# Attention layer of a two-layer graph network: the normalised rows are summed by the attention weights first, W is applied to the sums, and s is formed from the rows and W's row sums on VectorE

## The chip, the cores and the metric

The kernel runs on one NeuronCore of a Trainium2 chip. The core has five engines, each with its own in-order queue of instructions: TensorE (PE in the profile; matmuls and transposes, with weight loads shown as PEld), VectorE (DVE), ScalarE (ACT), GpSimd (POOL) and SyncE (SP, which here only issues loads). Engines wait for one another on semaphores. The metric is the device time of the whole program in microseconds, the median of the runs.

## What is computed

The input x has 128 graphs of 128 nodes with 256 features, all in float32, and adj gives each graph's 128 x 128 adjacency as integers. Two layers follow each other, both with a normalisation ahead and a residual sum behind:

```
h = relu(layernorm(x));  x = x + GRU_layers(h, adj)      # layer 0
h = relu(layernorm(x));  x = x + attention(h, adj, W)    # layer 1
```

Layer 0 repeats a gated update three times: messages h @ weight[i] are summed over neighbours (A transposed), and a GRU cell combines the sums with h. Layer 1 is

```
Wh      = h @ W
s       = Wh.sum(axis=-1)
e       = leaky_relu(s[:, :, None] + s[:, None, :], 0.2);  e = -inf where adj == 0
alpha   = softmax(e, axis=-1)
h_prime = alpha @ Wh
```

The kernel uses that alpha @ Wh can have its division by the softmax's denominator at the end, together with the residual sum.

## The kernel before

Graphs are worked on in groups of G = 4, so there are 32 groups. A group's data is kept in two layouts: rows (nodes on the partitions) and T (features on the partitions, in KD = 2 halves of 128). `normed` (L137) normalises four 128 x 256 row blocks: statistics on VectorE, the reciprocal root on GpSimd (L145, L146), the scaling on VectorE (L149). `rows_to_T` (L153) and `T_to_rows` (L175) transpose on TensorE, eight transposes each. `aggregate` (L185) sums rows over neighbours and leaves the sum in T layout; VectorE evicts it. `gru_half` (L207) computes one half of the new state: four gate sums in PSUM, of twelve 512-wide matmuls, then sigmoid and tanh on ScalarE and five operations on VectorE, the last of which writes hT (L226). W of the three message layers is folded into the gate weights ahead of the loop.

`group` (L228) is a generator: it yields after each step of a group, and 16 steps make a group. Step 11 (L253 to L257) forms x1, the input of the attention layer, and normalises it; step 12 transposes it with the Relu in the eviction; step 13 multiplies by W, evicts the product `wh` with ScalarE and reduces it to s; step 14 (L266 to L283) builds the scores and the softmax; step 15 transposes the weights to eT; step 16 forms the output and stores it.

Two streams take the even and the odd groups. The first is started LAG = 7 steps early; then each is advanced by one step in turn (L309 to L316), so that the vector work of one stream's attention falls beside the gate matmuls of the other. From the code in that sequence the framework's scheduler makes the order of each engine's queue when the program is built: it moves instructions past each other where their data allow it. On the chip each queue then runs in that order. PSUM has five buffers for gates and three for everything else, `ps_misc` (L57); the tiles of the pool `work` have three buffers unless a number is given. Loads go through SyncE's queue two groups ahead, stores through GpSimd's.

## Time and profile before

| | |
|---|---|
| median of 3 runs | 2614.0 us (2613.59 to 2614.19) |
| profiled execution | 2614.36 us, of which 2612.6 us lie between the first and the last instruction (the span) |
| TensorE busy | 2547.0 us, 97% of the span |
| VectorE busy | 1282.0 us, 49% |
| ScalarE busy | 720.8 us, 28% |
| GpSimd busy | 104.1 us, 4% |
| mean granted TensorE clock | 0.994 of full |

In a row of the page or of the groups, the text ahead of the bar names the line, the engine, the operation, what it writes and reads (`out<-in`) with shapes, and how often it occurs; behind the bar stand the busy time in us and the mean duration of one in ns, and then the idle time of the engine just ahead of these instructions with what ended it. In a timeline a row gives the start and length in us, the engine, the line, the operation and how many were merged, and in brackets the idle time ahead of it and what ended that. In a table of stretches, each row gives a stretch, its length, the busy time and count of PE, PEld, DVE, ACT and POOL, the granted clock, the share of the DMA engines and GB/s. A float32 matmul leaves two records, a transpose one. The ends of matmuls are modelled, and neighbouring matmuls overlap in the records.

### The profile page before, as it was taken

Reading aid. Unit: us, or ns where it says so; the run is one execution under the profiler, and the core shown is the slowest. Engines: PE = TensorE matmul, PEld = TensorE weight load, DVE = VectorE, ACT = ScalarE, POOL = GpSimd, SP = SyncE. Lnnn points to the kernel's source line nnn. Section 1 sums busy time; section 2 is a strip of 40 time slices with the busy share of each in tenths; the row PEclk is TensorE's granted clock in tenths of the full one; section 3 lists DMA queues with packets and bytes.
Section 4 is the critical chain, followed back from the end, with each engine's and each line's share of the span. In section 5 each row is a group of like instructions: output and inputs, shape, how many; then the busy total and the mean of one; then the engine's idle time right before and its main releaser. Section 6 shows DMA issues by size and latency. Waiting matters only on the chain.

```text
span 2612.6 us, 22325 instructions
## 1 busy us (share of the span) xinstructions
PE 2547.0 (97%) x8532; PEld 1357.0 (52%) x8532; DVE 1282.0 (49%) x2487; ACT 720.8 (28%) x1063; POOL 104.1 (4%) x166
## 2 busy tenths in 40 slices
PE   6999999999999999999999999999999999999996
PEld 4455555555555555555555555555555555555553
DVE  3355454555545455454554545555454554545544
ACT  1223222332222322222232223322223222222322
POOL 0000000000000000000000000000000000000000
PEclk9999999999999999999999999999999999999998
DMA  3000000000000000000000000000000000000000
GB/s 101 1 21 21 9 21 20 15 18 12 17 21 21 13 21 13 16 21 13 20 21 9 21 21 15 19 13 17 21 21 12 21 9 16 17 9 8 9 1 17
DMA packets 42700, 46.01 MB, mean 18 GB/s; under 512 B 3168, under 2 KB 38496, under 8 KB 42592
## 3 DMA queue, kind: packets, MB, share of 16 engines
q1 hardware_dynamic: 33792, 25.17, 3.2%
q0 software_dynamic: 4608, 16.78, 1.8%
q10 hardware_dynamic: 4192, 2.63, 0.4%
q8 instruction: 67, 1.10, 0.2%
q14 instruction: 41, 0.34, 0.0%
HBM read 27.79 MB, written 16.78 MB: 17 GB/s over the span
## 4 chain that ended last, share of the span: by engine, by line
PE 87%; DVE 6%; issue 2%; ACT 2%; POOL 1%; DMA 1%; ACTq 0%; POOLq 0%; DVEq 0%
PE gate L203 69%; PE misc L191 7%; PE misc L170 4%; PE misc L181 3%; PE misc L294 2%; DVE h L149 1%; DVE bn_st L141 1%; POOL rstd L146 1%; PE misc L159 1%; ACT z L222 1%; DVE hT L226 1%; DVE d L225 1%; ACT L222 1%; PE misc L268 1%; PE misc L128 0%
## 5 line engine op out<-in xcount | busy, mean ns | idle before, releaser
L203 PE MATMUL gate<-hT,w_hhT 128*128 128x512 f32 x2304 | 1096.5, 593 | 0.0
L203 PE MATMUL gate<-aT,w_x 128*128 128x512 f32 x2304 | 1093.5, 596 | 0.0
L203 PEld LDWEIGHTS gate<-aT,w_x 128*128 128x128 f32 x2304 | 427.4, 190 | 553.7 <-issue 477.5
L203 PEld LDWEIGHTS gate<-hT,w_hhT 128*128 128x128 f32 x2304 | 419.2, 191 | 431.3 <-issue 407.2
L215 DVE SCALAR_TENSOR_TENSOR u<-gate,bias_h,r 128x512 f32<-128x512 f32 x192 | 144.0, 750 | 417.7 <-PE gate L203 417.7
L212 ACT ACTIVATE r<-gate,bias_s 128x512 f32<-128x512 f32 x192 | 132.1, 688 | 726.0 <-PE gate L203 726.0
L219 ACT ACTIVATE n<-u,bias_i 128x512 f32<-128x512 f32 x192 | 138.8, 723 | 610.8 <-DVE u L217 540.8
L225 DVE TENSOR_TENSOR d<-d,z 128x512 f32<-128x512 f32 x192 | 132.6, 691 | 238.1 <-ACT z L222 236.5
L222 ACT ACTIVATE z<-gate,bias_s 128x512 f32<-128x512 f32 x192 | 131.8, 687 | 272.4 <-PE gate L203 271.0
L191 PEld LDWEIGHTS misc<-a,rows 128*128 128x128 f32 x1536 | 185.4, 193 | 17.4 <-issue 11.6
L224 DVE TENSOR_TENSOR d<-hT,n 128x512 f32<-128x512 f32 x192 | 131.9, 687 | 124.0 <-ACT n L219 123.9
L191 PE MATMUL misc<-a,rows 128*128 128x128 f32 x1536 | 188.4, 276 | 0.0
L217 DVE TENSOR_TENSOR u<-u,gate 128x512 f32<-128x512 f32 x192 | 131.3, 684 | 116.2 <-PE gate L203 115.8
L193 DVE COPY aT<-misc 128x512 f32<-128x512 f32 x192 | 130.0, 684 | 40.0 <-PE misc L191 39.7
L181 PE MATMUL misc<-ident,hT 128*128 128x128 f32 x768 | 119.9, 278 | 22.1 <-DVE hT L226 16.9
L226 DVE TENSOR_TENSOR hT<-n,d 128x512 f32<-128x512 f32 x192 | 132.3, 689 | 4.4
L181 PEld LDWEIGHTS misc<-ident,hT 128*128 128x128 f32 x768 | 87.6, 141 | 75.4 <-DVE hT L226 48.3
L170 PE MATMUL misc<-w,h1T 128*128 128x256 f32 x512 | 121.6, 386 | 0.6 <-ACT h1T L160 0.5
L170 PEld LDWEIGHTS misc<-w,h1T 128*128 128x128 f32 x512 | 95.7, 192 | 24.8 <-issue 7.2
L250 ACT COPY rows<-misc 128x512 f32<-128x512 f32 x128 | 69.1, 591 | 100.7 <-PE misc L181 100.7
L262 DVE TENSOR_REDUCE s<-wh 128x4 f32<-128x1024 f32 x32 | 39.0, 1220 | 109.3 <-ACT wh L172 109.3
L300 POOL DMA_DIRECT2D out_dram<-o x32 | 25.6, 802 | 1296.7 <-DVE o L297 1259.5
(60 smaller groups left out, 1201.1 us busy)
## 6 DMA issues: line engine op xcount, KB each, us to landing
xt<-in_x_dram SPq DMA_DIRECT2D x32, 512.0 KB, 3.9
out_dram<-o POOLq DMA_DIRECT2D x32, 512.0 KB, 3.4
at<-in_adj_dram SPq DMA_DIRECT2D x32, 256.0 KB, 2.8
w_msg<-in_L_gnn_weight_dram ACTq DMA_DIRECT2D x1, 768.0 KB, 7.0
w_hh_nat<-in_L_gnn_w_hh_dram ACTq DMA_DIRECT2D x1, 768.0 KB, 10.6
w_ih_nat<-in_L_gnn_w_ih_dram ACTq DMA_DIRECT2D x1, 768.0 KB, 13.8
w<-in_L_gnn_W_dram ACTq DMA_DIRECT2D x1, 256.0 KB, 9.0
bias_i<-in_L_gnn_b_ih_dram ACTq DMA_DIRECT2D x1, 3.0 KB, 11.8
```

The lines of the kernel that those rows point to most:

```text
L170: nc.tensor.matmul(ps[:, b, :], srcT[:, k, (b0 + b) * N:(b0 + b + 1) * N], w[:, k, :], start=(k == 0), stop=(k == KD - 1))
L181: nc.tensor.transpose(ps[:, b, k * P:(k + 1) * P], srcT[:, k, (b0 + b) * N:(b0 + b + 1) * N], ident)
L191: nc.tensor.matmul(ps[:, b * N:(b + 1) * N], m[:, b, k * P:(k + 1) * P], a[:, b, :], start=True, stop=True)
L203: nc.tensor.matmul(ps, w[:, k, c * P:(c + 1) * P], t[:, k, :], start=(i == 0), stop=(i == n - 1))
L212: nc.scalar.activation(r, p_r, AF.Sigmoid, bias=bias_s[:, cr:cr + 1])
L215: nc.vector.scalar_tensor_tensor(u, p_hn, bias_h[:, cn:cn + 1], r, op0=OP.add, op1=OP.mult)
L217: nc.vector.tensor_tensor(u, u, p_in, OP.add)
L219: nc.scalar.activation(n, u, AF.Tanh, bias=bias_i[:, cn:cn + 1])
L222: nc.scalar.activation(z, p_z, AF.Sigmoid, bias=bias_s[:, cz:cz + 1])
L224: nc.vector.tensor_tensor(d, hT[:, j, :], n, OP.subtract)
L225: nc.vector.tensor_tensor(d, d, z, OP.mult)
L226: nc.vector.tensor_tensor(new[:, j, :], n, d, OP.add)
```

## The change

At the start the sums of W's rows over its outputs, `w1_out`, are reduced on VectorE, and transposed and copied into `w1_sum`, which holds them in a row on all partitions. In the attention layer h1 gets its Relu in place on ScalarE and is no longer transposed; s is formed on VectorE, graph by graph, as the sum over a row of h1 times `w1_sum`. After the softmax, `aggregate` sums the rows of h1 by eT and leaves the sums in T layout, and `rows_product` multiplies those by W straight into the PSUM tile that the output step reads. The step that transposed h1 and the step that formed `wh` are gone, the summing is a step of its own, and s joins the step of the normalisation: 15 steps make a group. The numbers of the lines behind the change move up by 7 or so.

```diff
+    w1_out = const.tile([P, KD], F32, name="w1_out")
+    nc.vector.tensor_reduce(w1_out, w1, AX.X, OP.add)
+    w1_sum = const.tile([P, D], F32, name="w1_sum")
+    ps = ps_misc.tile([P, 512], F32, name="misc")
+    for k in range(KD):
+        nc.tensor.transpose(ps[:, k * P:(k + 1) * P], w1_out[:, k:k + 1].to_broadcast([P, P]), ident)
+    nc.scalar.copy(w1_sum, ps[:, :D])
...
-    def rows_to_T(src, name, bufs, func=AF.Copy):
+    def rows_to_T(src, name, bufs):
...
-            nc.scalar.activation(dst[:, k, :], ps[:, :GN], func)
+            nc.scalar.copy(dst[:, k, :], ps[:, :GN])
...
-    def rows_product(srcT, w, name):
-
-        dst = work.tile([P, G, D], F32, name=name)
-        for b0 in range(0, G, 2):
-            ps = ps_misc.tile([P, 2, D], F32, name="misc")
-            for b in range(2):
-                for k in range(KD):
-                    nc.tensor.matmul(ps[:, b, :], srcT[:, k, (b0 + b) * N:(b0 + b + 1) * N],
-                                     w[:, k, :], start=(k == 0), stop=(k == KD - 1))
-            nc.scalar.copy(dst[:, b0:b0 + 2, :], ps)
-        return dst
+    def rows_product(srcT, w, b0):
+
+        ps = ps_misc.tile([P, 2, D], F32, name="misc")
+        for b in range(2):
+            for k in range(KD):
+                nc.tensor.matmul(ps[:, b, :], srcT[:, k, (b0 + b) * N:(b0 + b + 1) * N],
+                                 w[:, k, :], start=(k == 0), stop=(k == KD - 1))
+        return ps
...
-        h = normed(x1, "h")
-        yield
-        h1T = rows_to_T(h, "h1T", 2, AF.Relu)
-        yield
-        wh = rows_product(h1T, w1, "wh")
+        h1 = normed(x1, "h")
+        nc.scalar.activation(h1, h1, AF.Relu)
         s = small.tile([P, G], F32, name="s")
-        nc.vector.tensor_reduce(s, wh, AX.X, OP.add)
+        for b in range(G):
+            hw = work.tile([P, D], F32, name="hw")
+            nc.vector.scalar_tensor_tensor(hw, h1[:, b, :], 1.0, w1_sum, op0=OP.mult, op1=OP.mult,
+                                           accum_out=s[:, b:b + 1])
         yield
...
         nc.scalar.copy(eT, p_e)
         yield
+
+        hT = aggregate(h1, eT)
+        yield
         o = work.tile([P, G, D], F32, name="o")
         for b0 in range(0, G, 2):
-            ps = ps_misc.tile([P, 2, D], F32, name="misc")
-            for b in range(2):
-                nc.tensor.matmul(ps[:, b, :], eT[:, b0 + b, :], wh[:, b0 + b, :],
-                                 start=True, stop=True)
+            ps = rows_product(hT, w1, b0)
```

## The prediction

> **What bounds the kernel now.** I read the page's busy shares first, then its groups.

> ```profile
> PE 2547.0 (97%) x8532; PEld 1357.0 (52%) x8532; DVE 1282.0 (49%) x2487; ACT 720.8 (28%) x1063; POOL 104.1 (4%) x166
> ...
> L203 PE MATMUL gate<-hT,w_hhT 128*128 128x512 f32 x2304 | 1096.5, 593 | 0.0
> ...
> L262 DVE TENSOR_REDUCE s<-wh 128x4 f32<-128x1024 f32 x32 | 39.0, 1220 | 109.3 <-ACT wh L172 109.3
> ```

> TensorE (PE) is busy almost throughout, VectorE (DVE) half the time. So time is PE's work plus PE's stalls. The 593 ns overlap each other; the spacing comes from the timeline of PE:

> ```profile
> 1242.51 1.04 PE L181 MATMUL misc<-ident,hT 128*128 128x128 f32 x8
> 1243.39 1.88 PE L203 MATMUL gate<-hT,w_hhT 128*128 128x512 f32 x4
> 1245.11 1.88 PE L203 MATMUL gate<-aT,w_x 128*128 128x512 f32 x4
> ...
> 1257.33 0.87 PE L181 MATMUL misc<-ident,hT 128*128 128x128 f32 x6 [0.97 <-DVE hT L226]
> 1258.04 3.19 PE L170 MATMUL misc<-w,h1T 128*128 128x256 f32 x14
> 1261.07 1.95 PE L191 MATMUL misc<-a,rows 128*128 128x128 f32 x16
> ...
> 1362.84 1.89 PE L294 MATMUL misc<-wh,eT 128*128 128x256 f32 x8
> 1364.57 0.27 PE L181 MATMUL misc<-ident,hT 128*128 128x128 f32 x1
> ...
> 1415.95 0.87 PE L181 MATMUL misc<-ident,hT 128*128 128x128 f32 x6 [0.97 <-DVE hT L226]
> ```

> From start to start: eight transposes 0.87 us, four 512-wide records 1.72 (0.429 each; a matmul leaves two records), 16 records of L191 1.78, eight of L294 1.73, L170's 14 3.03 (0.216 each). The same stall stands at 1257.33 and 1415.95: two groups take 158.62 us, one 79.31.

> PE's work per group: gates 144 x 0.429 = 61.8; L191 3 x 1.78 = 5.3; L181 3 x 0.87 = 2.6; L159 2 x 0.87 = 1.7; L170 3.45; L294 1.73; L268 and L286 0.87. Sum 77.5, so stalls cost 1.8 per group.

> What decides the changed kernel is DVE at that stall, from its timeline:

> ```profile
> 1243.15 0.69 DVE L254 TENSOR_TENSOR x<-xt,misc 128x512 f32<-128x512 f32 x1 [1.64 <-PE misc L181]
> ...
> 1248.66 1.38 DVE L149 TENSOR_SCALAR h<-x,bn_mv,rstd 128x256 f32<-128x256 f32 x4 [1.12 <-POOL rstd L146]
> 1249.96 0.75 DVE L215 SCALAR_TENSOR_TENSOR u<-gate,bias_h,r 128x512 f32<-128x512 f32 x1
> ...
> 1253.97 0.41 DVE L149 TENSOR_SCALAR h<-xt,bn_mv,rstd 128x256 f32<-128x256 f32 x1 [1.40 <-POOL rstd L146]
> ...
> 1256.59 0.69 DVE L226 TENSOR_TENSOR hT<-n,d 128x512 f32<-128x512 f32 x1
> ```

> One stream's normalisation stands in DVE's queue ahead of the other stream's GRU update. That update's hT ends 14.77 us after the transposes of x1 began (1257.28 less 1242.51), though its gate sums were done at 11.2. Before, 3.8 us of attention work filled the time.

> [...] L273 reads one f32 tile twice and takes 683 ns, as a plain tensor_tensor (688)[...]. [...] after 3.36 idle us before 46.30 the clock column (after POOL's) fell.

> ```profile
> 46.00:48.00 2.00, 1.70 (x14) 1.71 (x15) 1.99 (x7) 1.25 (x3) 0.00 (x0) 0.89 0.03 8
> 48.00:50.00 2.00, 2.00 (x11) 2.00 (x11) 0.69 (x1) 1.36 (x2) 0.00 (x0) 0.50 0.59 163
> 50.00:52.00 2.00, 2.00 (x7) 1.10 (x7) 0.69 (x1) 0.00 (x0) 0.00 (x0) 0.76 0.77 230
> ```

> [...]

> **The change part by part.** *PE work.* Gone: eight transposes of h1 (0.87) and L294 (1.73). Added: a second aggregation of 16 records (1.78). The product with W (3.45) moves behind it. Net -0.82: 76.7 per group, -26 us in all.

> *ScalarE (ACT) work.* Four evictions of 0.59 go, one Relu of 1.07 comes; ACT is 28% busy, so only its place counts.

> *DVE work.* The reduction (1.22) goes; two evictions of 0.69 and four weighted row sums come. A row sum: 128x256 takes 0.41 alone (L149), each waits for the one before (dependent steps are 0.72 apart for 0.69 of work, so 0.03), and I add 0.08 for the accumulator read (the small aggregations follow each other at 0.07). 0.52 each, 2.08 together. Bounds: 1.6 (overlapped, 0.33 + 0.07)[...].

> *Order.* A group now has 15 steps in place of 16, with the lag at 7, so the streams pair anew. In the built order (what each engine's queue of the changed kernel holds) every group has the same stretch on PE: eight transposes of x1; a gate half of the other stream (10.30); four transposes of s; two transposes and four gate records that need only the first half of the other stream's hT; six transposes that need its second half; four gate records; four transposes of e; the aggregation. The product that used to stand there is gone. DVE's order there: x1, statistics, h, u of L215, row sums, L217, rest of the next group's statistics, its h, e plus the row of s, d times z, e plus the column, hT, then the rest of the softmax. The queues of SyncE and GpSimd keep their order, with the same loads, reciprocal roots and stores.

> *First stall,* counted from the start of x1's transposes. As before, h ends at 7.53 and L215 at 8.2. Relu ends at 8.64; two statistics end at 8.84. Row sums 8.76 to 10.84 (PE needs s at 11.17: just hidden, by the gate half). L217 to 11.5; last statistics and aggregation to 12.15; 1.40 through GpSimd, as at 1253.97, to 13.55; three h 1.05 to 14.6; then four operations (e, d, e, hT) at 0.60 steps: hT ends at 17.0. PE has finished s (0.44), two transposes (0.22) and four gate records (1.72) at 11.17 + 2.38 = 13.55. Stall: 3.5. Waiting behind those transposes: the other stream's next aggregation and all its gates.

> *Second stall.* From the six transposes PE has 0.65 + 1.72 = 2.37 of work. The softmax's exp stands in ACT's queue behind the two row copies those transposes feed: they end 1.66 after the first transpose (1257.33 to 1258.99), table load 1.28, exp 0.63, the mask product 0.69 on DVE, 0.1 of handovers: e is ready after 4.36. Stall: 2.0. Before, these transposes came a whole gate half later.

> *The rest.* The eviction behind the aggregation costs some 0.2 per group, as similar ones do now. The aggregation with eT has 6.9 us of gate work ahead of it and the product 10.3, so their evictions are hidden; without that cover, 0.7 each.

> *Sum.* 76.7 + 0.2 + 3.5 + 2.0 = 82.4 per group against 79.3: +3.1 for 31 groups = 97. The last has no partner: -0.8. Start: the transposes of W's sums stand first on PE, and their reduction ahead of all weight copies on DVE. W was issued at 12.54 and took 9.0 to land: 21.5, reduction 0.7. Then 24 weight transposes at the slow 0.213 take 5.1, so the message weights start at about 28, not 22.46: +5.5. Tail: s comes about 6.5 earlier, aggregation, eviction and product cost about 6 more: 0. Together +102 on a span of 2612.6, in a run of 2614.36; the median is 2614.0. Forecast 2716.

> **The rivals.** *Clock or row sums dearer.* The first stall nears the idle time that halved the clock once. That slow stretch cost 1.6 us (12 records of L191 at 0.213, not 0.111, and 0.4 after). In every group it is +50[...]. Either gives 2760 to 2766. Against: [...]the second stall absorbs part of a slow stretch.

> *First stall half as long:* DVE catches up by 1.7 us, 2663. For it: I sum twenty DVE steps. Against: 14.77 was measured for the shorter chain, and 2.08 plus two steps of 0.60 come on top.

> *Faster.* If hT is there at 13.55, only the second stall is left: 76.7 + 0.2 + 2.0 = 78.9, -0.4 x 31 - 0.8 + 5.5 = -8: 2606. It decides below some 2.2 us of stall per group, that is with hT up to 0.2 after 13.55. Against: hT came at 14.77 without the new DVE work.

> *The change doesn't save what it says:* PE's saving is 0.82 per group by the spacing, and gone if the second aggregation costs 2.60. Its form is L191's, so I hold that excluded.

> **How the numbers follow.** Two stalls as summed 0.66; clock or row sums 0.16; half stall 0.11; faster 0.05; no change within 0.2% (some 5 us, what this measurement can tell) 0.02. Slower is 0.93. The forecast's own spread is about 25 us (0.4 per stall). The range, 2672 to 2780, takes in cheap row sums (-15) with that spread, and the dear cases with some of it; the half stall, faster and equal cases lie mostly outside.

> **What would show it** (lines of the changed file). Right: L188 waits about 3.5 us on hT (L233) in each of 31 groups, L293 about 2.0 on e (L285); group spacing 82.4; row sums near 0.5; first weight transposes near 22. Wrong: no wait at L188; row sums far from 0.5; a granted clock below 0.97; a wait at L275 on s.

## The result, and the profile after

The changed kernel takes 2719.6 us (median of 5 runs, 2718.4 to 2720.5), the kernel before 2614.15 beside it: a ratio of 1.040, 95% interval 1.039 to 1.042. It is slower by 105 us, though its TensorE has less to do. The busy shares on the page after:

```profile
PE 2551.2 (94%) x8534; PEld 1367.6 (50%) x8534; DVE 1327.1 (49%) x2776; ACT 690.1 (25%) x968; POOL 116.9 (4%) x166
```

PE's busy time has hardly moved (2547.0 before), and its share fell from 97% to 94%: the new time is idle time. Among the groups of instructions, the new row sums have two rows, the multiplication and the read of its accumulator; the reciprocal root on GpSimd, 1019 ns before, has become slower:

```profile
L156 POOL TENSOR_TENSOR rstd<-rstd,neghalf 128x4 f32<-128x4 f32 x64 | 78.0, 1219 | 5.0
...
L268 DVE SCALAR_TENSOR_TENSOR hw<-h,w_sum 128x256 f32<-128x256 f32 x128 | 46.5, 425 | 1.6 <-ACT h L264 1.6
...
L268 DVE DVE_READ_ACCUMULATOR hw<-h,w_sum 128x1 f32 x128 | 11.7, 91 | 0.0
```

The waits say what PE stood still for (total us, how often, the longest):

```profile
PE misc L188 <- DVE hT L233: 95.7, 34, 3.1
...
PE misc L293 <- DVE e L285: 29.8, 28, 5.2
```

The kernel before had 16.9 us of the first kind (18 times, at its L181). In the timeline of PE, one group after the change:

```profile
1386.17 0.60 PE L275 MATMUL misc<-ident,s 128*128 128x128 f32 x4
1386.60 0.38 PE L188 MATMUL misc<-ident,hT 128*128 128x128 f32 x2
1386.82 1.88 PE L210 MATMUL gate<-hT,w_hhT 128*128 128x512 f32 x4
1391.77 0.88 PE L188 MATMUL misc<-ident,hT 128*128 128x128 f32 x6 [3.06 <-DVE hT L233]
1392.48 1.88 PE L210 MATMUL gate<-hT,w_hhT 128*128 128x512 f32 x4
1396.24 0.63 PE L293 MATMUL misc<-ident,e 128*128 128x128 f32 x4 [1.88 <-DVE e L285]
1396.70 1.95 PE L198 MATMUL misc<-a,rows 128*128 128x128 f32 x16
```

These are the two stalls of the prediction. The same six transposes stood at 1309.44 in the group before, so the spacing is 82.33 us there, against 79.31 before the change. The four gate records behind 1386.82 take 1.72 us from start to start, so PE was free at 1388.54: the first stall is 3.23. The second is 1396.24 less 1394.20, 2.04. The records' own idle times are about 0.16 shorter, because the ends of matmuls are modelled. In VectorE's timeline of the same stretch one sees what PE waited for:

```profile
1383.75 0.41 DVE L268 SCALAR_TENSOR_TENSOR hw<-h,w_sum 128x256 f32<-128x256 f32 x1
1384.08 0.09 DVE L268 DVE_READ_ACCUMULATOR hw<-h,w_sum 128x1 f32 x1
...
1385.12 0.69 DVE L224 TENSOR_TENSOR u<-u,gate 128x512 f32<-128x512 f32 x1
1385.72 0.43 DVE L151 BATCH_NORM_STATS2 bn_st<-xt 128x6 f32<-128x256 f32 x1
1386.06 0.37 DVE L153 BATCH_NORM_AGGREGATE bn_mv<-bn_st 128x2 f32<-128x6 f32 x4
1386.66 0.69 DVE L231 TENSOR_TENSOR d<-hT,n 128x512 f32<-128x512 f32 x1 [0.23 <-ACT n L226]
1388.25 1.06 DVE L159 TENSOR_SCALAR h<-xt,bn_mv,rstd 128x256 f32<-128x256 f32 x3 [0.90 <-POOL rstd L156]
1389.22 0.68 DVE L278 TENSOR_TENSOR e<-e,misc 128x512 f32<-128x512 f32 x1
1389.82 0.69 DVE L232 TENSOR_TENSOR d<-d,z 128x512 f32<-128x512 f32 x1
1390.42 0.69 DVE L279 TENSOR_TENSOR e<-e,s 128x512 f32<-128x512 f32 x1
1391.02 0.69 DVE L233 TENSOR_TENSOR hT<-n,d 128x512 f32<-128x512 f32 x1
```

Four row sums take 1.37 us, from 1383.75 to L224 at 1385.12. Behind d (L231) VectorE stands still 0.90 us for GpSimd, does three h of the next group, which nobody needs yet, and two sums of e, before hT comes. GpSimd, in its own timeline, was slower at the second root than at the first:

```profile
1380.07 1.03 POOL L156 TENSOR_TENSOR rstd<-rstd,neghalf 128x4 f32<-128x4 f32 x1
...
1386.79 1.43 POOL L156 TENSOR_TENSOR rstd<-rstd,neghalf 128x4 f32<-128x4 f32 x1
```

The sum of the 105 us: the spacing, 3.02 in each of 31 groups, is 94; the TensorE clock, lowered after the stall in 24 of 30 groups (mean granted clock 0.976, 0.994 before), adds about 12 (see the third run); the start adds 2.5 (first gate record at 52.86, not 50.33); the end gives back 2.3 (33.2 us from the last two transposes of a state to the end, not 35.5); the last group's shorter work gives 0.8.

### The profile page after: what moved, and what is told of

It is laid out like the page before. It is cut to its first block, busy times and chain, and to the rows that moved or that the text cites. A ratio compares the mean times of both kernels' runs of the same rounds, so it can differ in the third digit from the quotient of the medians.

```text
span 2717.5 us, 22493 instructions
## 1 busy us (share of the span) xinstructions
PE 2551.2 (94%) x8534; PEld 1367.6 (50%) x8534; DVE 1327.1 (49%) x2776; ACT 690.1 (25%) x968; POOL 116.9 (4%) x166
## 4 chain that ended last, share of the span: by engine, by line
PE 75%; DVE 14%; POOL 3%; ACT 3%; issue 3%; DMA 1%; POOLq 0%; SPq 0%; ACTq 0%
PE gate L210 58%; PE misc L198 8%; PE misc L178 4%; POOL rstd L156 3%; PE misc L188 3%; DVE bn_st L151 3%; DVE h L159 2%; DVE hw L268 2%; DVE d L232 2%; DVE hT L233 1%; ACT L284 1%; PE misc L169 1%; ACT rows L257 1%; PE misc L293 1%; DVE x L261 1%
## 5 line engine op out<-in xcount | busy, mean ns | idle before, releaser
L210 PE MATMUL gate<-hT,w_hhT 128*128 128x512 f32 x2304 | 1120.6, 607 | 0.0
L210 PE MATMUL gate<-aT,w_x 128*128 128x512 f32 x2304 | 1082.3, 594 | 0.0
L210 PEld LDWEIGHTS gate<-hT,w_hhT 128*128 128x128 f32 x2304 | 427.9, 195 | 441.3 <-issue 411.4
L222 DVE SCALAR_TENSOR_TENSOR u<-gate,bias_h,r 128x512 f32<-128x512 f32 x192 | 144.2, 751 | 586.7 <-PE gate L210 485.1
L226 ACT ACTIVATE n<-u,bias_i 128x512 f32<-128x512 f32 x192 | 138.9, 723 | 573.0 <-DVE u L224 573.0
L200 DVE COPY aT<-misc 128x512 f32<-128x512 f32 x256 | 176.2, 688 | 91.6 <-PE misc L198 91.6
L188 PE MATMUL misc<-ident,hT 128*128 128x128 f32 x768 | 115.2, 289 | 95.7 <-DVE hT L233 95.7
L231 DVE TENSOR_TENSOR d<-hT,n 128x512 f32<-128x512 f32 x192 | 132.9, 692 | 145.8 <-ACT n L226 145.8
L224 DVE TENSOR_TENSOR u<-u,gate 128x512 f32<-128x512 f32 x192 | 132.3, 689 | 118.7 <-PE gate L210 115.4
L188 PEld LDWEIGHTS misc<-ident,hT 128*128 128x128 f32 x768 | 94.1, 148 | 144.3 <-DVE hT L233 123.2
L233 DVE TENSOR_TENSOR hT<-n,d 128x512 f32<-128x512 f32 x192 | 132.0, 687 | 2.3
L178 PE MATMUL misc<-w,aT 128*128 128x256 f32 x512 | 116.2, 380 | 0.0
L178 PEld LDWEIGHTS misc<-w,aT 128*128 128x128 f32 x512 | 97.6, 191 | 26.5 <-issue 14.8
L156 POOL TENSOR_TENSOR rstd<-rstd,neghalf 128x4 f32<-128x4 f32 x64 | 78.0, 1219 | 5.0
L155 POOL TENSOR_TENSOR rstd<-bn_mv,eps 128x4 f32<-128x4 f32 x64 | 12.5, 196 | 1490.0 <-DVE bn_mv L153 1490.0
```

The lines of the kernel that those rows point to most:

```text
L156: nc.gpsimd.tensor_tensor(rs, rs, neghalf, OP.pow)
L178: nc.tensor.matmul(ps[:, b, :], srcT[:, k, (b0 + b) * N:(b0 + b + 1) * N], w[:, k, :], start=(k == 0), stop=(k == KD - 1))
L188: nc.tensor.transpose(ps[:, b, k * P:(k + 1) * P], srcT[:, k, (b0 + b) * N:(b0 + b + 1) * N], ident)
L200: nc.vector.tensor_copy(aT[:, k, :], ps[:, :GN])
L210: nc.tensor.matmul(ps, w[:, k, c * P:(c + 1) * P], t[:, k, :], start=(i == 0), stop=(i == n - 1))
L222: nc.vector.scalar_tensor_tensor(u, p_hn, bias_h[:, cn:cn + 1], r, op0=OP.add, op1=OP.mult)
```

## The experiments

Each was timed beside the kernel before, whose median lay between 2612.5 and 2613.4. Differences in us are to the changed kernel's 2719.6 unless said otherwise. "Stall" is from start to start, "idle" as recorded.

### 1. The row sums taken out

A copy of each row's first feature stands in for s, so the weighted sums are left out of the computation.

```diff
-        for b in range(G):
-            hw = work.tile([P, D], F32, name="hw")
-            nc.vector.scalar_tensor_tensor(hw, h1[:, b, :], 1.0, w1_sum, op0=OP.mult, op1=OP.mult,
-                                           accum_out=s[:, b:b + 1])
+        nc.vector.tensor_copy(s, h1[:, :, 0])
```

> The changed kernel without the row sums: s is a copy of each row's first feature, so the scores are not the reference's; all else stays, and the order on TensorE is the same. Theory (the chain on VectorE ahead of hT sets the first stall): the four row sums take 1.37 us of that chain, the copy about 0.1, so the wait of L188's six transposes falls from 3.2 to about 1.9 us in each of 31 groups, the wait on e stays at 2.0, and with idle time under 2 us the clock stays at 1.0. 2720 - 39 - 12 = about 2668 (2655 to 2680). Rival 1 (the loss is the new pairing of the steps alone, the row sums lie in spare time of VectorE): no change, 2715 to 2722. Rival 2 (the slower clock is the loss): the clock recovers and only some 12 us come back.

Measured 2689.9 us, ratio 1.030 (1.028 to 1.031): 30 less, not the 50 expected. The first stall fell to 2.40 us, but its idle time in PE's timeline was still long:

```profile
1294.08 1.48 PE L188 MATMUL misc<-ident,hT 128*128 128x128 f32 x6 [2.24 <-DVE hT L233]
```

Two things were not foreseen. The scheduler changed VectorE's order when the sums were gone (d went between the first and the other three h of the next group). And these six transposes have a length of 1.48, not 0.88: the clock was down after the idle time, as in 18 of the groups. The spacing is 81.5 where the clock stayed full and up to 82.0 where not. So the row sums are part of the stall, but taking them out doesn't remove it.

### 2. The row sums done twice

```diff
-        for b in range(G):
+        for b in (0, 1, 2, 3, 0, 1, 2, 3):
             hw = work.tile([P, D], F32, name="hw")
```

> The changed kernel with the four row sums computed twice; same order on TensorE. Theory: the chain ahead of hT grows by 1.37 us; s comes 1.37 later against a slack of 0.7, so L275 waits about 0.65 and L188 about 3.9 to 4.0, together 1.37 more than before; the idle time is longer, so the clock falls in every group. 2720 + 42 + 5 to 30 = 2767 to 2792. Rival 1 (row sums lie in spare time): 2720.

Measured 2698.7 us, ratio 1.033 (1.031 to 1.035): 21 us *less* with more work. Eight sums took 2.75 us, as expected (1291.27 to L224 at 1294.02). The rest of VectorE's timeline tells why it was faster:

```profile
1295.55 0.69 DVE L231 TENSOR_TENSOR d<-hT,n 128x512 f32<-128x512 f32 x1 [0.23 <-ACT n L226]
1296.16 0.68 DVE L278 TENSOR_TENSOR e<-e,misc 128x512 f32<-128x512 f32 x1
1296.76 0.68 DVE L232 TENSOR_TENSOR d<-d,z 128x512 f32<-128x512 f32 x1
1297.36 0.68 DVE L279 TENSOR_TENSOR e<-e,s 128x512 f32<-128x512 f32 x1
1297.96 0.68 DVE L233 TENSOR_TENSOR hT<-n,d 128x512 f32<-128x512 f32 x1
...
1299.17 0.41 DVE L159 TENSOR_SCALAR h<-xt,bn_mv,rstd 128x256 f32<-128x256 f32 x1
```

When the program was built, the scheduler now put the next group's h behind hT. The wait for GpSimd and the three h are gone from the chain, and that is worth more than four more sums cost. The first stall is 2.45, in place of 3.23. The theory "longer row sums, longer stall" falls as a rule for the time: an edit of VectorE's work is also an edit of its order. That became the next theory: the next group's normalisation ahead of hT is the larger part.

### 3. The first wait filled with TensorE work

Twenty more transposes, whose results are overwritten, stand in the long wait.

```diff
                 for k in range(KD):
+                    for i in range(fill if b0 == b == 0 and k == 1 else 0):
+                        nc.tensor.transpose(ps[:, 0, P:2 * P], srcT[:, 0, b0 * N:(b0 + 1) * N], ident)
                     nc.tensor.transpose(ps[:, b, k * P:(k + 1) * P],
```

> The changed kernel with 20 extra transposes per group on TensorE, written into a place that the next real transpose overwrites, put into the wait for hT (they read the half of hT that is there already); the eight gate records around it are then split otherwise (two before the wait, six behind). Theory (VectorE's chain sets when the six transposes and then the transposes of e start, and the idle TensorE loses its clock in most groups): the 2.2 us of extra work are free, the wait on hT falls to about 1.9 and that on e to about 1.1, a group still takes 82.3 us, and the clock stays at 1.0, which gives back the 12 us of slow clock: 2707 (2700 to 2712). Rival (TensorE's work bounds this stretch): 20 x 0.109 x 31 = 68 us more, 2785. Rival (the clock falls for another reason than idle time): 2720 with the clock at 0.976.

Measured 2708.3 us, ratio 1.036 (1.035 to 1.038), as expected: 11 us less with more for TensorE to do. The mean clock rose from 0.976 to 0.995 and the groups are 82.31 us apart, all of them within 0.02. So the slow clock costs 11 us of the 105; nearly all the rest is the stalls themselves.

### 4. The row sums alone, in the kernel before

Relu on ScalarE, the weighted sums and the sums of W go into the kernel before; h1 is transposed and multiplied by W as before, in 16 steps.

```diff
         h = normed(x1, "h")
+        nc.scalar.activation(h, h, AF.Relu)
+        s = small.tile([P, G], F32, name="s")
+        for b in range(G):
+            hw = work.tile([P, D], F32, name="hw")
+            nc.vector.scalar_tensor_tensor(hw, h[:, b, :], 1.0, w1_sum, op0=OP.mult, op1=OP.mult,
+                                           accum_out=s[:, b:b + 1])
         yield
-        h1T = rows_to_T(h, "h1T", 2, AF.Relu)
+        h1T = rows_to_T(h, "h1T", 2)
...
-        nc.vector.tensor_reduce(s, wh, AX.X, OP.add)
```

> The kernel before with one part of the change alone: s comes from the Relu'd rows times W's row sums on VectorE (the reduction of wh goes), while h1 is still transposed and multiplied by W first; 16 steps, and the order on TensorE nearly as before. Theory (the new pairing takes the cover away, the row sums only lengthen the chain): of two groups one has the place where hT is late; its wait of 1.1 us grows by the 1.4 us of row sums and perhaps 0.4 behind GpSimd, the other is covered by the product; 15.5 x 1.4 to 1.8 = 22 to 28, and 2 to 3 for the later start: 2614 + 24 to 31 = 2638 to 2645. Rival 1 (row sums are the whole loss): 2700 or more. Rival 2 (pairing alone): 2614 to 2618.

Measured 2644.1 us, ratio 1.012 (1.010 to 1.013): 31 more than the kernel before, within what was expected. In its waits the old stall is longer, 2.1 us where it was 0.97:

```profile
PE misc L189 <- DVE hT L234: 34.0, 18, 2.1
```

As before the change this stands once in two groups. That the time met the expectation is partly luck: 15 stalls longer by 1.12 make 17 us, not the 22 to 28 expected, and some 10 come from the clock, which fell in six of the 15 pairs of groups (161.4 us each where most others take 159.7). So about 30 of the 105 us come with the row sums in the old order of steps; the rest comes with the second part of the change, which takes the product with W out of the first wait and pairs the streams anew. The first run, which has that part without the row sums, fits this: it is 77 us above the kernel before.

### 5. The next group's normalisation queued later on VectorE

Nothing is computed differently. The next group's normalisation, its statistics and GpSimd's root included, is put behind the softmax reciprocal of the same stream's group before it. This is an order of VectorE's queue and adds no wait on another engine.

```diff
-        y = normed(xt, "h")
+        held = tc.issue_after(soft[g % 2].ins) if g >= 2 else nullcontext()
+        with held:
+            y = normed(xt, "h")
...
-        nc.vector.reciprocal(rden, den)
+        soft[g % 2] = nc.vector.reciprocal(rden, den)
```

> Only the order on VectorE is changed: the first layer's normalisation of a group (the three h, which wait for GpSimd's second root) is queued behind the same stream's softmax reciprocal of the group before, so it no longer stands ahead of hT in the long wait. My theory (the wait is the length of VectorE's queue ahead of hT, and what stands in it by accident of the order counts as much as the new row sums): hT ends 2.1 us earlier after the T8 transposes' start than in the changed kernel (0.90 of wait and about 1.2 of h), the first stall falls from 3.2 to about 1.1 us, the second stays at 2.0, the TensorE clock stays full in nearly every group, and the time is 2640 to 2665 us. Rival (the row sums' own chain and GpSimd's roots bound the wait, the next group's h only fills idle time of VectorE): the first stall stays above 2.7 us and the time within 2700 to 2722.

Measured 2638.7 us, ratio 1.010 (1.008 to 1.011): 81 less, a little below the range expected. PE's timeline:

```profile
1346.42 0.60 PE L279 MATMUL misc<-ident,s 128*128 128x128 f32 x4
1346.86 0.38 PE L188 MATMUL misc<-ident,hT 128*128 128x128 f32 x2
1347.07 1.88 PE L210 MATMUL gate<-hT,w_hhT 128*128 128x512 f32 x4
1349.97 0.87 PE L188 MATMUL misc<-ident,hT 128*128 128x128 f32 x6 [1.01 <-DVE hT L233]
1350.68 1.88 PE L210 MATMUL gate<-hT,w_hhT 128*128 128x512 f32 x4
1354.43 0.63 PE L297 MATMUL misc<-ident,e 128*128 128x128 f32 x4 [1.88 <-DVE e L289]
```

The first wait is 1.01 us of idle time in place of 3.06, the second is unchanged, the spacing is 80.08 and the clock stays full. In VectorE's timeline d starts as long after x1 as it did in the changed kernel, within 0.1 us; the gain lies behind it, where the wait for GpSimd and the three h stood. The larger part of the first stall, 2.05 us, was the place of work that isn't urgent. The mean of the root at L156 is back at 1017 ns.

### 6. The first sum of e queued behind hT as well

```diff
-        nc.vector.tensor_tensor(e, e, p_s, OP.add)
+        with tc.issue_after(state[0].ins):
+            nc.vector.tensor_tensor(e, e, p_s, OP.add)
```

Here `state[0]` is the instruction that last wrote a half of hT; the edit of the fifth run stays.

> As the run before, and the first sum of e is queued behind the other stream's hT as well. My theory: nothing but the new chain stands ahead of hT; the first stall goes to about 0 to 0.3 us, the second grows to about 2.3, and the time is 2615 to 2640 us. Rival (the queue is not it): 2690 or more.

Measured 2662.3 us, ratio 1.019 (1.017 to 1.020): 24 *more* than the fifth run, and above the range. The stalls did what was expected: 0.3 us at hT, and at e

```profile
1365.83 0.63 PE L298 MATMUL misc<-ident,e 128*128 128x128 f32 x4 [2.38 <-DVE e L290]
```

But one idle time of 2.38 cost more than two of 1.01 and 1.88. Of every three groups two are 81.34 us apart and one 79.70. The 1.64 between them are gate and aggregation records at the lowered clock; 20 such groups make 33 us, and 2662 less 33 is 2629, inside the range expected.

### 7. Only the pairing of the steps

One empty step ahead of e's transposes, and the aggregation and the product made one step, still 15 in all; no order is forced on VectorE.

```diff
+        yield
         p_e = ps_misc.tile([P, G, N], F32, name="misc")
...
         hT = aggregate(h1, eT)
-        yield
         o = work.tile([P, G, D], F32, name="o")
```

> Only the pairing of the two streams' steps is changed: one empty step ahead of e's transposes, and aggregation and product made one step. My theory (the second stall is e's transposes standing behind only 2.37 us of TensorE work of the other stream): the second stall goes to under 0.4 us, the first stays at about 3.2, and the time is 2650 to 2670 us, 50 to 70 below the changed kernel. Rival (the stall is only a lag of VectorE that comes back elsewhere): the sum of both stalls stays within 0.5 us of 5.3 and the time at 2700 or more.

Measured 2693.6 us, ratio 1.031 (1.029 to 1.032): 26 less, not 50 to 70. The second stall is gone as foreseen. The first is 3.23 as foreseen, so the groups should be some 80.3 apart; they are 81.92. A table of 2 us stretches across the first stall has the rest:

```profile
1374.00:1376.00 2.00, 2.00 (x11) 1.23 (x9) 0.95 (x5) 1.03 (x2) 1.59 (x2) 1.00 0.00 0
1376.00:1378.00 2.00, 0.53 (x2) 0.00 (x0) 1.92 (x5) 0.00 (x0) 0.04 (x1) 1.00 0.00 0
1378.00:1380.00 2.00, 0.40 (x2) 0.41 (x3) 2.00 (x4) 0.00 (x0) 0.00 (x0) 0.74 0.00 0
1380.00:1382.00 2.00, 2.00 (x8) 1.48 (x7) 1.75 (x4) 1.40 (x3) 0.00 (x0) 0.50 0.00 0
1382.00:1384.00 2.00, 2.00 (x15) 1.60 (x15) 0.39 (x1) 1.69 (x2) 0.00 (x0) 0.90 0.00 0
```

The clock falls to half (0.50) within the idle time and stays there into the work behind it. It does so in all 30 intervals between groups, and the mean clock is 0.977. In the changed kernel the second stall took up part of this, since a slow PE only arrives later at a wait; here nothing does.

### 8. Both orders and the pairing together

The edits of the fifth, sixth and seventh runs.

> Both orders on VectorE and the re-pairing together. My theory, by which the two stalls are all that the change costs and its TensorE work is less than before: stalls of 0.2 to 0.6 us a group, 77.0 to 77.5 us a group, 2540 to 2570 us, below the kernel before by 2 to 3 per cent. Rival (a lag of VectorE that returns at another step): 2600 us or more.

Measured 2558.3 us, ratio 0.979 (0.978 to 0.980): 161 less than the changed kernel and 55 less than the kernel before, as expected. The busy shares, and the transposes of e in PE's timeline:

```profile
PE 2503.7 (98%) x8534; PEld 1343.0 (53%) x8534; DVE 1328.9 (52%) x2776; ACT 684.6 (27%) x968; POOL 103.9 (4%) x166
```

```profile
1318.88 1.88 PE L210 MATMUL gate<-hT,w_hhT 128*128 128x512 f32 x4
1320.60 1.88 PE L210 MATMUL gate<-aT,w_x 128*128 128x512 f32 x4
1322.31 0.60 PE L299 MATMUL misc<-ident,e 128*128 128x128 f32 x4
```

No idle time stands ahead of e, none above 0.13 us anywhere in the group; the spacing is 77.44. VectorE does all that it did in the changed kernel. So VectorE was never short of time there: what cost was the order of its work and the pairing, which left PE too little to do behind it.

### 9. Pairing, with twenty transposes in the wait

The edits of the third and seventh runs together, to tell whether the 1.6 us of the seventh are the clock.

> The re-pairing run with 20 more transposes (0.109 us each, 2.17 us) put into its long wait, as in the run that filled the changed kernel's wait. The re-pairing run missed its expectation: its second stall is gone, yet its groups stand 81.92 us apart, where work 76.76, stall 3.23 and small gaps 0.3 make 80.3. My theory (the rest, 1.6 us a group, is TensorE at its slow clock after the idle 3.06 us): with the idle time cut to about 1 us the spacing is 80.2 to 80.4 and the time 2638 to 2648 us, although TensorE does more. Rival (a lag of VectorE that returns in small gaps): the spacing stays at 81.9 and the time at 2690 or above.

Measured 2680.0 us, ratio 1.026 (1.024 to 1.027): between the two expectations, so it settles nothing by its time. The clock is full (0.995), but the spacing is 81.39. The timeline shows a side effect: with so many transposes ahead, the scheduler had moved two of the four gate records behind hT, so 0.86 us of real work came out of the wait. (In the third run the same had happened, and its second stall had absorbed it: 1.18 instead of 2.04.)

### 10. The kernel before with its own order mended

To tell how much of the eighth run is the change and how much the order: in the kernel before, the next group's h is queued behind the other stream's hT.

```diff
         h = normed(x1, "h")
         yield
+        soft[g % 2] = state[0]
...
-        y = normed(xt, "h")
+        held = tc.issue_after(soft[g % 2].ins) if g >= 2 else nullcontext()
+        with held:
+            y = normed(xt, "h")
```

> The kernel before, with the next group's three h queued on VectorE behind the other stream's hT, the same kind of edit as in the best run, to tell how much of that run's gain is the change's and how much the order's. My theory: the wait of 0.97 us at the six transposes goes, up to 0.5 us comes back because the sums of W's output and the aggregation's evictions stand behind h now; 78.2 to 78.9 us a group and 2578 to 2602 us, so that the changed kernel in its best order is still 20 to 45 us below it, about 0.82 us of TensorE work a group. Rival (the order alone is what made the best run fast): 2565 us or less. Other rival (the stall only moves): 2606 or more.

Measured 2596.0 us, ratio 0.993 (0.992 to 0.995), inside the range of the theory. The stall of 0.97 is gone, two groups take 68.77 + 88.66 = 157.43 us, 78.7 each. The eighth run is 38 us below it. So with the mended orders tried here the change is worth 38 us, of which 0.82 us of TensorE work in each of 32 groups makes 26; how much an even better order of the kernel before would give was not tried.

### 11. The sums of W later at the start

The eighth run, with the reduction of W, its transposes and the eviction behind the setup of the message weights.

> The best run with the sums of W's columns (the reduction, two transposes, one eviction) put behind the message weights' setup in place of ahead of it. My theory, from the 2.5 us by which the first gate matmul came later in the changed kernel than before: 1.5 to 3 us less, 2555 to 2557 us. Rival (the start is hidden): within 1 us of 2558.

Measured 2554.1 us, ratio 0.977 (0.976 to 0.979): 4.2 less, more than expected and the fastest of all. The first gate record starts at 50.03 in place of 53.90. The expectation had been taken from the changed kernel, where it came at 52.86 because the aggregation ahead of it ran at full clock; in the eighth run the same sixteen records ran slow (3.31 us long, not 1.95).

### 12. Pairing, with twelve transposes in the wait

> The re-pairing run with 12 more transposes in its long wait in place of 20. With 20, the clock was full but the groups stood 81.39 us apart, since two records of the other stream's four gate matmuls had been moved behind hT, so the wait was 0.9 us longer than without the fill. With 12 all four stay ahead of hT. My theory (the re-pairing run lost 1.6 us a group to the slow clock and nothing else): idle 1.75 us, full clock, 80.2 to 80.5 us a group, 2637 to 2652 us. Rival (the clock is not it; VectorE's lag holds the spacing): 81.4 or more a group, 2675 or more.

Measured 2652.6 us, ratio 1.016 (1.014 to 1.017), 0.6 above the edge of the range; spacing 80.53, 0.03 above. All four gate records are ahead of hT again. The same table of stretches across this run's first wait:

```profile
1357.00:1359.00 2.00, 2.00 (x8) 0.75 (x5) 1.71 (x5) 0.00 (x0) 0.26 (x1) 1.00 0.00 0
1359.00:1361.00 2.00, 0.25 (x3) 0.19 (x3) 2.00 (x4) 0.00 (x0) 0.00 (x0) 1.00 0.00 0
1361.00:1363.00 2.00, 2.00 (x14) 1.52 (x14) 1.97 (x4) 1.59 (x3) 0.00 (x0) 1.00 0.00 0
```

hT comes as late as in the seventh run, PE does more, and it takes 41 us less: 1.39 us a group were the clock and nothing else. That explains all but 0.2 us a group of the seventh run's miss, for which there is no account. The sixth's is explained by the same sign in its trace, though there no run was made with the wait filled.

## Why the prediction was right

Forecast 2716, measured 2719.6. Taking its own steps:

**PE work**, 77.5 to 76.7: right. The medians of start to start of every kind of record, times their number in a group, give 77.57 before and 76.76 after.

**First stall**, 3.5: measured 3.23, and the place, the engine and the instruction waited for are those named. Two of its terms were off and nearly cancelled. The row sums were put at 0.52 each, with 1.6 for all four as the lowest bound; they took 0.34 each, 1.37 together, below that bound; by the prediction's own signs ("row sums far from 0.5") this term was wrong. The read of the accumulator, 91 ns long, stands beside the next main instruction and not behind it, so nothing is added for it, and the sums overlap, 0.34 us apart for 0.42 of length, as the scalings of L159 do (0.32 apart, 0.41 long). That row sums could be dearer, one of the rivals, was the author's estimate, and no run showed it. Against the low cost, the stretch through GpSimd was put at 1.40 "as at 1253.97"; from the end of the aggregation at 1386.43 to h at 1388.25 it is 1.82, because the second root took 1.43 in place of 1.03. hT ends 16.72 after the start of x1's transposes; 17.0 was forecast. That the two errors nearly cancel is luck.

**Second stall**, 2.0: measured 2.04. The chain from the six transposes through the row copies, the table load (1.28 us), exp and the mask product to the transposes of e is 4.47 us, against 4.36 and a handover.

**The rest**, 0.2: about 0.3. **Sum**, 82.4 a group: 82.33.

**Start**, +5.5: the message weights came at 28.29, as computed, but the first gate record only 2.5 later than before. The step ended at the message weights and took the rest as unchanged; but the first product of the message weights took 5.43 us, not 7.16, and the sixteen records of the first aggregation ran at full clock (1.95 us) where those of the kernel before ran slow (3.31). **Tail**, 0: -2.3. Both errors made the forecast too high, by 5 us together.

**The clock** was a rival at 1.6 us in every group, and zero in the forecast. It was neither: 24 of 30 groups show a stretch at lowered clock, but the second stall hid most of each, and 11 to 12 us are left. The argument against the rival, that the second stall absorbs part of a slow stretch, held (the seventh run, without the second stall, paid in every group). That the clock would stay full behind a stall of 3.5 us was not shown, and the trace of the kernel before did not support it: of the 3.36 us ahead of 46.30 only 2.17 lay in the 3.41 us whose end at 47.55 brought the fall (the last section has the lines). The mean clock, 0.976, came close to the 0.97 that the prediction named as a sign of being wrong.

So the number came out 4 us low, with terms of -12 (clock), +5 (start and tail) and +3 (spacing) around it; so close a number is luck in part. (Of the +3, one is a slip: 3.1 for 31 groups is 96, not 97.) The mechanism was right at both stalls. What the prediction did not see is that the first stall need not be there. It counted the wait for GpSimd and the three h in its chain but took VectorE's order as given; the runs show that of the chain ahead of hT the next group's normalisation holds 2.05 us, against 1.37 for the row sums, and that the order is nothing that the change needs. Of the rivals neither the half stall nor the faster case came.

## What to carry to other kernels

When one engine runs several streams' work in order, look at each stall of the busiest engine for what stands ahead of the awaited instruction and isn't urgent: here a wait for a third engine and three scalings of the next group, worth more than the new work itself. An edit of one operation can make the scheduler reorder its neighbours, so compare the queues of both programs before reading the difference of times as the price of the operation. And TensorE's idle time was not linear in cost here: a single wait of 2.38 us (run 6, mean clock 0.981) was dearer than two of 1.01 and 1.88 (run 5, 0.996), because the clock fell behind it in 20 of 30 groups.

## What the runs showed of the hardware

**The clock fell within the groups of every run whose longest idle time there was 2.1 us or more, and of none where it was 1.88 or less.** The longest single idle time of each run's groups, in how many of 30 intervals between groups a slow stretch of over 0.3 us stood (the last, without a partner, is left out), and the mean granted clock of the profiled execution:

| run | longest idle, us | intervals with a slow stretch | mean clock |
|---|---|---|---|
| before, and runs 10, 8 and 11 | 0.97, 0.34, 0.13, 0.13 | 0 | 0.994, 0.994, 0.995, 0.995 |
| runs 3, 9, 12 | 1.74, 1.74, 1.75 | 0 | 0.995, 0.995, 0.995 |
| run 5 | 1.88 | 0 | 0.996 |
| run 4 | 2.1 | 6 | 0.991 |
| run 1 | 2.24 | 18 | 0.984 |
| run 2 | 2.28 | 8 | 0.989 |
| run 6 | 2.38 | 20 | 0.981 |
| changed kernel | 3.06 | 24 | 0.976 |
| run 7 | 3.06 | 30 | 0.977 |

Between 1.88 and 2.1 us lies a border in these runs. Above it, where the idle time lay decided. The traces also record each change of the granted clock: 294 in the 14 traces (5 before, 51 in the changed kernel), and within a trace all are whole multiples of 3.41333 us apart, to 0.005 us over some 2600. So within a trace the changes keep to one grid. Cut into stretches of 3.41 us by this grid, called windows here, the traces have 10,535 windows at full clock. Behind 147 of them the clock fell; PE's records filled at most 1.40 us of each of these, with one exception (1.57, in run 4), and at least 1.40 of each of the other 10,388. In the traces of the two kernels alone it is 28 falls in 1,498 windows, with at most 1.38 us of work ahead of a fall and at least 1.53 elsewhere. Two stalls of the changed kernel show it, idle for 3.06 and 3.07 us. The first is cut by the end of a window at 1390.09, so that at most 1.68 us of it lie in one window, and the clock stays at 1.00. Of the second 2.24 us lie in one window, which holds 1.18 us of work, and the next runs at half:

```profile
1390.09:1393.51 3.42, 1.74 (x9) 1.27 (x10) 3.38 (x7) 1.14 (x3) 0.00 (x0) 1.00 0.00 0
1393.51:1396.92 3.41, 1.53 (x8) 0.73 (x8) 1.94 (x4) 1.86 (x3) 0.00 (x0) 1.00 0.00 0
...
1553.93:1557.35 3.42, 1.18 (x3) 0.19 (x1) 2.68 (x6) 0.00 (x0) 0.70 (x1) 1.00 0.00 0
1557.35:1560.76 3.41, 2.58 (x8) 2.01 (x9) 2.99 (x6) 1.57 (x3) 0.00 (x0) 0.50 0.00 0
```

The fall in the kernel before, at the start, is of the same kind:

```profile
44.13:47.55 3.42, 1.25 (x11) 1.26 (x12) 3.42 (x11) 1.62 (x3) 0.00 (x0) 1.00 0.02 5
47.55:50.97 3.42, 3.42 (x16) 3.12 (x15) 1.53 (x4) 1.81 (x3) 0.00 (x0) 0.50 0.63 180
```

**GpSimd's power of a 128x4 tile** took 1.03 us, and 1.43 where it ran beside VectorE's d (L231): at 1386.79 in the changed kernel, while in the fifth run the two roots took 1.03 and 1.01. Beside all 30 slow roots of the changed kernel VectorE ran d and nothing else, and beside the 34 fast ones it ran nothing; in the kernel before, 15 roots ran beside a copy (L193) and took 1.03 too. No run moved d alone, so the cause of the 1.43 was not shown.

**A multiply with an accumulated row sum** on VectorE, 128x256 in float32, took 0.34 us from one to the next in the changed kernel (four from 1383.75 to L224 at 1385.12: 1.37), where they don't depend on each other, near to the scaling of the same shape (four of L159 from 1381.14 to L222 at 1382.43 in the changed kernel: 1.29, or 0.32 each).
